# Causal Toeplitz filters: one quarter by three block products, both lags in one matmul, with the second layer's work in other steps

## The chip, the cores and the metric

The kernel runs on one core of a Trainium2 chip. The metric is the device time of one execution in microseconds (us), median of repeated runs. The core's engines each have an instruction queue of their own, taken in order: TensorE (PE, matmuls; PEld is its load of weights), VectorE (DVE), ScalarE (ACT), GpSimd (POOL) and SyncE (SP, which only issues DMAs here). They wait for each other by semaphores. Everything is float32.

## The reference

Two "metaformer" layers on x of shape (8, 128, 32, 32), so 8 images of 1024 tokens with 128 channels. What matters here is the token mixer of layer 0 and what comes after it:

```python
x = x + attention(ln_c(x))                    # layer 0, first half
t = to_tokens(x)
t = t + stu(ln_t(t))                          # layer 0, second half: the filters
x = from_tokens(t)
x = x + deformable_conv(ln_c(x))              # layer 1, first half: gathers
t = t + experts(ln_t(t))                      # layer 1, second half: top 2 of 8 experts

def stu(u):                                   # for 4 resolutions, mixed by weights
    U_plus  = causal_convolution(phi_k, u)            # 16 filters k, each over all tokens
    U_minus = sgn * causal_convolution(phi_k, sgn * u)  # sgn = +1, -1, +1, ...
    out = sum_k s_k * (U_plus_k @ Mpp_k + U_minus_k @ Mpm_k)
    return out + sum_{i<3} shift(u, i) @ Mu_i
```

With the signs, the sum and the difference of U_plus and U_minus need only tokens of equal or of unequal parity. So tokens are split into even and odd ones, 512 of each, and a filter into its even and its odd lags. One filter then is, for each image, four causal convolutions of length 512: from each source parity to each result parity. Each is a product with a lower triangular Toeplitz matrix of 512 x 512.

## The kernel before

The kernel has three stages: attention (to about 911 us), the filters with the second layer of earlier images beside them (to about 2743 us), and the second layer of the last two images alone.

**Filter stage** (`spectral_and_second_layer`). Images go in four groups of two. The loop runs over 64 items of work, (group, filter k) with 16 filters to a group. One iteration does the convolutions of its own item and the mix of the item before. For each of the 4 pairs (result parity, term) and each of 2 images, `filter_image` (L1366 to L1378) computes a convolution by four matmuls into one PSUM bank `pu`: the weights are a tile of 128 source tokens (`ur`, of which `xc` and `ht` are other names in the even groups), the moving operand is a piece of the filter's Toeplitz rows (`teto`, or `hk` for the first filter), of 512, 384, 256 and 128 columns. That is the lower triangle in 10 blocks of 128 x 128. ACT copies the bank to `us` (L1378). Two banks take turns as `pu`.

`mix` multiplies the `us` of the item before by its matrices `mf` and accumulates in four banks `po` (L1362), for 512 columns after each image's convolution. The mix is cut in SPANS, since the four resolutions reach over different numbers of tokens. At a group's first filter `start_sums` begins `po` with the residual and the three lags `mu`. At its last, `finish` copies `po` to `x2`.

In the first group, `load_matrices` makes `mf` from M_plus and M_minus: a sum and a difference on POOL (L1274, L1275), four weightings on DVE (L1279, L1281), and a write to HBM, from where later groups load it. `lags` makes `mu` in the same way (L1248, L1250).

**Work beside it.** The second layer of the previous group's two images, and the preparation of the next group, are generators in a list `behind`. After each image's convolution and piece of mix, `advance(2.6)` takes steps from the list until they add up to that many units (a step that yields no number counts 1). So what order the engines' queues have is written out by hand. A step's instructions stand in the queue of each engine behind all that came ahead in the program. An image's steps are: transposes back to tokens, norm (`norm_steps`: statistics on DVE, an inverse root by Newton steps on POOL, scaling on DVE, L793), a matmul with the convolution's matrices (L1015), its result written to a table in HBM (24 DMAs from SP), `corners` (indices and weights of the bilinear samples), 24 points, each an indirect DMA on POOL (L1065) and four multiply-adds on DVE (L1078), a norm, `gates` (the top two experts), and 16 expert steps of one matmul (L1096) and four multiply-adds on DVE (L1102). Next comes the preparation of the next group: load, norm, and `channels` (p_ut, L1318). What is left of it at the group's end is done at once.

In the last stage, the two images of the last group run the same steps, interleaved with each other (`alone`).

**What sets buffers free.** The filter tile `teto` has three buffers, `mf` three, the gathered rows `g` nine.

Of the kernel before, what the change touches and what calls it, by code (L numbers as in the profile page):

```python
# [34 lines left out]
GROUPS = ((0, 1), (2, 3), (4, 5), (6, 7))  # L35
RATE = (2.6, 3.5)
STAGGER = 16
# [363 lines left out]
class BoundedAttention:  # L401
# [6 lines left out]
    def __init__(self, nc, cp):  # L408
        self.nc = nc
        HG, NH = self.HG, self.NH  # L410
        self.xc = cp.tile([P, T], F32, name="xc")
        self.ht = cp.tile([P, NT, C], F32, name="ht")
        self.hk = cp.tile([P, 2 * HT + 2], F32, name="hk")
        self.wq = cp.tile([C, HG, NH, 32], F32, name="wq")
        self.wk = cp.tile([C, HG, NH, 32], F32, name="wk")
        self.wv = cp.tile([C, C], F32, name="wv")
        self.group = cp.tile([P, NG], F32, name="group")
        self.spread = cp.tile([P, 2, P], F32, name="spread")
        self.pick = cp.tile([P, HG, NH, HD], F32, name="pick")
# [381 lines left out]
class DeformAndExperts:  # L801
# [182 lines left out]
    def image(self, b, x2, alone):  # L984
# [8 lines left out]
        hc = sb.tile([C, T], F32, tag="hc", name="hc")  # L993
        yield from self.turn_steps(ht, hc)
        yield

# [48 lines left out]
        idx, w = got  # L1045
        nc.gpsimd.tensor_tensor(tok, tok, self.cb.unsqueeze(1).to_broadcast([P, NT, C]), ALU.add)
        x3 = sb.tile([P, NT, C], F32, tag="x3", name="x3")
# [6 lines left out]
        def fetch():  # L1054
            if len(fetched) < len(points):
                i, tap = points[len(fetched)]
                if alone:
                    at = idx[:, i, tap : tap + 1]
                else:
                    if tap == 0:  # L1060
                        here.append(sb.tile([P, TAPS], I32, tag="here", name="here", bufs=3))
                        nc.scalar.copy(here[-1], idx[:, i, :])  # L1062
                    at = here[-1][:, tap : tap + 1]
                g = sb.tile([P, 4 * C], F32, tag="g", name="g", bufs=9)
                nc.gpsimd.indirect_dma_start(  # L1065
                    out=g, out_offset=None, in_=rows,
                    in_offset=bass.IndirectOffsetOnAxis(ap=at, axis=0),
                )
                fetched.append(g)

        for _ in range(3):
            fetch()
        yield
        yield
# [60 lines left out]
    def gates(self, tt, got):  # L1135
# [23 lines left out]
        yield  # L1159
        oh2 = self.first_max(e2, "b")  # L1160
        nc.vector.tensor_add(oh1, oh1, oh2)
        gates = sb.tile([P, P // NE, NE], F32, tag="gates", name="gates")
# [14 lines left out]


def read_filter(nc, t, phi_e, phi_o, k):
    nc.sync.dma_start(t[:, 0:HT], bass.AP(phi_e.tensor, k * PHI_ROW, [[1, P], [1, HT]]))  # L1180
    nc.sync.dma_start(
        t[:, HT : 2 * HT + 1], bass.AP(phi_o.tensor, k * PHI_ROW, [[1, P], [1, HT + 1]])
    )
    return t[:, 0:HT], t[:, HT : 2 * HT + 1]

# [32 lines left out]
class Spectral:  # L1218
# [4 lines left out]
    def __init__(self, ctx, tc, dram, phi_e, phi_o, M_u, M_plus, M_minus, coef, x1d, back, given):  # L1223
        nc = self.nc = tc.nc
        cp = ctx.enter_context(tc.tile_pool(name="s_const", bufs=1))
        self.sb = ctx.enter_context(tc.tile_pool(name="s_sb", bufs=1))
        self.up = ctx.enter_context(tc.tile_pool(name="s_u", bufs=2, space=PSUM))
        self.op = ctx.enter_context(tc.tile_pool(name="s_o", bufs=1, space=PSUM))
# [12 lines left out]

    def lags(self, w):
        nc = self.nc
        for f in range(NFR):
            m = self.sb.tile([C, TAPS, C], F32, tag="m_u", name="m_u")
            nc.sync.dma_start(m, self.M_u[f].rearrange("i d e -> d i e"))
            if f == 0:
                nc.vector.tensor_scalar(self.mu[:, f], m, w[:, f : f + 1], None, ALU.mult)  # L1248
            else:
                nc.vector.scalar_tensor_tensor(  # L1250
                    self.mu[:, f], m, w[:, f : f + 1], self.mu[:, f - 1], ALU.mult, ALU.add
                )

    def load_filter(self, k):


        t = self.sb.tile([P, 2 * HT + 1], F32, tag="teto", name="teto", bufs=3)
        return read_filter(self.nc, t, self.phi_e, self.phi_o, k)

    def load_matrices(self, k, first):  # L1260

        nc, sb = self.nc, self.sb
        mf = sb.tile([C, NFR, 2, C], F32, tag="mf", name="mf", bufs=3)
        if not first:
            nc.sync.dma_start(mf, self.mfd[k])
            return mf
        mp = sb.tile([C, NFR, C], F32, tag="mp", name="mp")
        mm = sb.tile([C, NFR, C], F32, tag="mm", name="mm")  # L1270
        nc.sync.dma_start(mp, self.M_plus[:, k].rearrange("f d e -> d f e"))
        nc.sync.dma_start(mm, self.M_minus[:, k].rearrange("f d e -> d f e"))
        both = sb.tile([C, NFR, 2, C], F32, tag="both", name="both")
        nc.gpsimd.tensor_add(both[:, :, 0, :], mp, mm)  # L1274
        nc.gpsimd.tensor_sub(both[:, :, 1, :], mp, mm)  # L1275
        for f in range(NFR):
            by = self.coef[:, f, k : k + 1]
            if f == 0:
                nc.vector.tensor_scalar(mf[:, f], both[:, f], by, None, ALU.mult)  # L1279
            else:  # L1280
                nc.vector.scalar_tensor_tensor(  # L1281
                    mf[:, f], both[:, f], by, mf[:, f - 1], ALU.mult, ALU.add
                )
        nc.sync.dma_start(self.mfd[k], mf)
        return mf

    def prepare(self, group):

        nc, sb = self.nc, self.sb
        group["x1"], group["ur"] = [], []  # L1290
        for n, b in enumerate(group["images"]):
# [7 lines left out]
            if group["number"] % 2:  # L1299
                group["ur"].append(sb.tile([P, NT, C], F32, tag="ur", name="ur", bufs=2))  # L1300
            else:
                group["ur"].append(self.given.ur[n])
        group["ut"] = sb.tile([C, 2, 2, HT + 1], F32, tag="ut", name="ut")

    def normal(self, group, newton):

        for x1, ur in zip(group["x1"], group["ur"]):
            yield from norm_steps(self.nc, self.sb, x1, ur, 1e-5, newton)

    def channels(self, group, bank):  # L1310
# [55 lines left out]

    def filter_image(self, group, n, par, term, teto, us):

        nc = self.nc
        src = par if term == 0 else 1 - par  # L1370
        flt = teto[0] if term == 0 else teto[1][:, par : par + HT]
        pu = self.up.tile([P, HT], F32, tag="u", name="pu")
        for i in range(4):
            nc.tensor.matmul(  # L1374
                pu[:, i * P : HT], group["ur"][n][:, src * 4 + i, :], flt[:, 0 : HT - i * P],
                start=(i == 0), stop=(i == 3),
            )
        nc.scalar.copy(us[:, n, :], pu)  # L1378

    def mix(self, group, par, term, spans, mf, us, last):  # L1380
        for lo, hi, k in spans:
            self.add(
                group, (par, lo // 256), self.span(group, par, lo, hi), mf[:, k - 1, term, :],
                us[:, 0 : len(group["images"]), lo:hi], last and term == 1,
            )
# [11 lines left out]
def spectral_and_second_layer(tc, spec, layer, weights):  # L1397
    groups = [{"images": im, "number": g} for g, im in enumerate(GROUPS)]
    work = [(g, k) for g in range(len(groups)) for k in range(NF)]
    spec.prepare(groups[0])  # L1400
    filters = {0: spec.given.filter, 1: spec.load_filter(1)}
    matrices = {0: spec.load_matrices(0, True)}
    spec.lags(weights)
    matrices[1] = spec.load_matrices(1, True)

# [16 lines left out]
    for n in range(len(work) + 1):  # L1422
# [9 lines left out]
        if now is not None and now[1] == 0 and now[0]:  # L1432
            for _ in starts[now[0]]:
                pass
        if n + 2 < len(work):
            filters[n + 2] = spec.load_filter(work[n + 2][1])
        sums = {}
        for i in range(4 if now or before else 0):
            par, term = divmod(i, 2)
            if now is not None:  # L1440
                group = groups[now[0]]
                us = spec.sb.tile([C, 2, HT], F32, tag="us", name="us", bufs=6)
                sums[i] = us
            for m in range(2):
                unit = now is not None and m < len(group["images"])
                if unit:
                    spec.filter_image(group, m, par, term, filters[n], us)
                if before is not None:
                    if before[1] == 0 and i + m == 0:
                        spec.start_sums(groups[before[0]])  # L1450
                    spec.mix(
                        groups[before[0]], par, term, SPANS[0:3] if m == 0 else SPANS[3:4],
                        matrices[n - 1], kept[i], before[1] == NF - 1,
                    )
                if unit:
                    advance(RATE[2 - len(group["images"])])
        if before is not None and before[1] == NF - 1:
            spec.finish(groups[before[0]])
        if n + 2 < len(work):
            matrices[n + 2] = spec.load_matrices(work[n + 2][1], work[n + 2][0] == 0)  # L1460
        kept, before = sums, now
    while behind:
# [106 lines left out]
```

## Time and profile before

| what | value |
|---|---|
| time, median of 3 runs | 2969.61 us (2966.56 to 2971.4) |
| span of the profiled run | 2966.7 us, 45298 instructions |
| PE busy | 2759.9 us, 93% |
| DVE, ACT, POOL busy | 1405.6, 982.0, 976.3 us |
| filter matmuls (L1374), share of the chain | 35% |
| mix and start of the sums (L1362), share of the chain | 16% |
| DMA | 199.80 MB, mean 67 GB/s |

The chain is the chain of work that ended last, followed back from the last instruction to whatever released each step. Busy time of PE overstates: its matmuls are pipelined and their ends are modelled, so the busy times of neighbours overlap. A matmul in float32 shows as two instructions.

The costliest rows that the change touches (line, engine, operation, tiles, count, busy us, mean ns of one, idle time of the engine before them and what ended it):

```profile
L1378 ACT COPY us<-pu 128x512 f32<-128x512 f32 x512 | 299.4, 585 | 1301.1 <-PE pu L1374 1266.9
...
L1374 PE MATMUL pu<-teto,ur 128*128 128x512 f32 (+3 forms) x2048 | 594.4, 433 | 0.0
...
L1078 DVE SCALAR_TENSOR_TENSOR x<-g,w,x 128x128 f32<-128x128 f32 x704 | 250.0, 356 | 43.0 <-DMA g<-tab,here 11.5
L1102 DVE SCALAR_TENSOR_TENSOR x<-p_e,gates,x 128x128 f32<-128x128 f32 x512 | 177.7, 350 | 188.7 <-PE p_e L1096 172.4
```

ACT sat idle ahead of the copies of `pu` until PE had written them: it waited for PE, not the other way round.

### The profile page before, as it was taken

What the parts mean: (1) busy time and instruction counts of PE and PEld (TensorE: products, weight loads), DVE (VectorE), ACT (ScalarE), POOL (GpSimd) and SP (SyncE); (2) the same over time, 40 slices, a digit from 0 to 9 for tenths busy, and PEclk for the clock granted to TensorE, in tenths of its full rate; (3) what the DMA queues carried; (4) which work ended last, traced back from release to release, by engine and by line L of the source; (5) the groups of instructions that cost most, each with busy time, mean ns of one, the idle gap of its engine ahead of it and who ended that gap; (6) DMA issues with size and microseconds to landing.
All of it is one profiled execution on the core that took longest, in us unless ns stands there. A gap on an engine that the chain in (4) does not pass through costs nothing.

```text
span 2966.7 us, 45298 instructions
## 1 busy us (share of the span) xinstructions
PE 2759.9 (93%) x18896; PEld 1693.4 (57%) x18896; DVE 1405.6 (47%) x2882; ACT 982.0 (33%) x1246; POOL 976.3 (33%) x977
## 2 busy tenths in 40 slices
PE   7999999999998999999999999999999999999316
PEld 3555555555555666666666666666666666666103
DVE  4888888888882200000432532333333153333586
ACT  4666667676661111112212111221211221221100
POOL 4777777777881211100200301210210030220230
PEclk9999999999998999999999999999999999999658
DMA  1000000000002322221614411521621441530730
GB/s 27 2 16 16 2 16 16 2 16 9 16 16 83 101 64 64 64 61 51 184 39 128 143 35 36 170 82 41 191 64 36 116 135 34 157 99 8 229 112 15
DMA packets 177012, 199.80 MB, mean 67 GB/s; under 512 B 17237, under 2 KB 135189, under 8 KB 176801
## 3 DMA queue, kind: packets, MB, share of 16 engines
q1 hardware_dynamic: 147328, 134.97, 15.3%
q0 software_dynamic: 16800, 55.59, 6.1%
q10 hardware_dynamic: 12672, 6.29, 0.7%
q8 instruction: 150, 2.46, 0.3%
q14 instruction: 62, 0.50, 0.1%
HBM read 128.88 MB, written 67.92 MB: 66 GB/s over the span
## 4 chain that ended last, share of the span: by engine, by line
PE 58%; DVE 6%; DMA 1%; issue 1%; POOL 0%; ACT 0%; SPq 0%; DVEq 0%; POOLq 0%; ACTq 0%
PE pu L1374 35%; PE po L1362 16%; PE p_e L1096 3%; DVE x L1078 2%; PE p_g L1015 1%; DVE x L1102 1%; DMA tab<-gs 1%; PE p_out L1113 0%; PE p_turn L918 0%; PE p_out L1116 0%; PE p_l L1140 0%; DVE st L785 0%; DVE mv L786 0%; PE p_ut L1318 0%; DMA g<-tab,cn_idx 0%
## 5 line engine op out<-in xcount | busy, mean ns | idle before, releaser
L1378 ACT COPY us<-pu 128x512 f32<-128x512 f32 x512 | 299.4, 585 | 1301.1 <-PE pu L1374 1266.9
L620 POOL TENSOR_TENSOR t<-e 128x1024 f32<-128x1024 f32 x256 | 607.9, 2375 | 199.4 <-ACT e L611 199.2
L648 DVE TENSOR_TENSOR e<-e,rb 128x2048 f32<-128x2048 f32 x256 | 570.8, 2279 | 83.6 <-PE rb L641 83.6
L1374 PE MATMUL pu<-teto,ur 128*128 128x512 f32 (+3 forms) x2048 | 594.4, 433 | 0.0
L611 ACT ACTIVATE e<-s 128x2048 f32<-128x2048 f32 x256 | 480.9, 1879 | 253.2 <-PE s L606 251.3
L1374 PEld LDWEIGHTS pu<-teto,ur 128*128 128x128 f32 x2048 | 386.5, 190 | 273.0 <-issue 185.1
L1362 PE MATMUL po<-us,mf 128*128 128x128 f32 (+2 forms) x2048 | 528.1, 381 | 0.0
L606 PE MATMUL s<-q,k 32*128 32x256 f32 x4096 | 296.1, 403 | 14.0 <-ACT e L611 13.2
L658 PE MATMUL av<-e,vt 128*32 128x256 f32 x4096 | 290.0, 391 | 2.9 <-DVE e L648 1.6
L1374 PE MATMUL pu<-teto,xc 128*128 128x512 f32 x992 | 290.5, 436 | 0.0
L1374 PE MATMUL pu<-teto,ht 128*128 128x512 f32 x992 | 287.7, 433 | 0.0
L1065 POOL DMA_INDIRECT g<-tab,here x144 | 137.6, 956 | 447.0 <-ACT here L1062 252.8
L1374 PEld LDWEIGHTS pu<-teto,xc 128*128 128x128 f32 x992 | 189.0, 191 | 153.9 <-issue 114.2
L1362 PEld LDWEIGHTS po<-us,mf 128*128 128x128 f32 x2048 | 270.9, 192 | 4.1 <-issue 3.9
L1078 DVE SCALAR_TENSOR_TENSOR x<-g,w,x 128x128 f32<-128x128 f32 x704 | 250.0, 356 | 43.0 <-DMA g<-tab,here 11.5
L1102 DVE SCALAR_TENSOR_TENSOR x<-p_e,gates,x 128x128 f32<-128x128 f32 x512 | 177.7, 350 | 188.7 <-PE p_e L1096 172.4
L606 PEld LDWEIGHTS s<-q,k 32*128 32x128 f32 x4096 | 186.4, 185 | 136.9 <-ACT e L611 115.7
L1374 PEld LDWEIGHTS pu<-teto,ht 128*128 128x128 f32 x992 | 187.7, 190 | 110.0 <-issue 64.7
L770 POOL TENSOR_SCALAR rs_v<-rs_v 128x8 f32<-128x8 f32 x18 | 4.4, 245 | 711.3 <-DVE rs_b L768 711.3
L658 PEld LDWEIGHTS av<-e,vt 128*32 128x32 f32 x4096 | 101.7, 109 | 141.4 <-issue 85.2
L1096 PE MATMUL p_e<-ew,tc 128*128 128x512 f32 x256 | 133.1, 626 | 15.4 <-DVE x L1102 10.3
L634 DVE RECIPROCAL r<-z 128x256 f32<-128x256 f32 x64 | 112.5, 1757 | 69.0 <-PE z L627 68.8
(237 smaller groups left out, 1829.0 us busy)
## 6 DMA issues: line engine op xcount, KB each, us to landing
tab<-gs SPq DMA_DIRECT2D x168, 256.0 KB
mf<-mfd SPq DMA_DIRECT2D x48, 512.0 KB
teto<-in_phi_o SPq DMA_DIRECT2D x63, 256.5 KB
teto<-in_phi_e SPq DMA_DIRECT2D x63, 256.0 KB
mfd<-mf SPq DMA_DIRECT2D x16, 512.0 KB
tab<-gs ACTq DMA_DIRECT2D x24, 256.0 KB
xc<-in_x SPq DMA_DIRECT2D x8, 512.0 KB
x1d<-xt SPq DMA_DIRECT2D x8, 512.0 KB
```

The source lines that it names most:

```text
L606: nc.tensor.matmul(s[:, j, c, :], img["k"][rows, hg, 2 * r + c, :], q[rows, qc * QU : (qc + 1) * QU], start=True, stop=True,)
L611: nc.scalar.activation(e.rearrange("p j c q -> p (j c q)"), s.rearrange("p j c q -> p (j c q)"), AF.Exp, scale=float(HD) ** -0.5,)
L620: nc.gpsimd.tensor_add(t, e[:, :, 0, :], e[:, :, 1, :])
L648: nc.vector.tensor_tensor(e, e, un["rb"].unsqueeze(2).to_broadcast([P, NH, 2, QU]), ALU.mult)
L658: nc.tensor.matmul(qrt["av"][32 * j : 32 * j + 32, 0:QU], img["v"][:, 2 * r + c, P * hg + 32 * j : P * hg + 32 * j + 32], un["e", r][:, j, ...
L1065: nc.gpsimd.indirect_dma_start(out=g, out_offset=None, in_=rows, in_offset=bass.IndirectOffsetOnAxis(ap=at, axis=0),)
L1078: nc.vector.scalar_tensor_tensor(x3[:, i, :], fetched[n][:, k * C : (k + 1) * C], w[:, i, tap, k : k + 1], (tok if tap + k == 0 else x3)[: ...
L1096: nc.tensor.matmul(pe, tc[:, i * P : (i + 1) * P], self.ew[:, grp * 4 : grp * 4 + 4, :].rearrange("d e c -> d (e c)"), start=True, stop=True,)
L1102: nc.vector.scalar_tensor_tensor(x3[:, i, :], pe[:, k * C : (k + 1) * C], gate[:, i, grp * 4 + k : grp * 4 + k + 1], x3[:, i, :], ALU.mult ...
L1362: self.nc.tensor.matmul(out, lhsT, rhs, start=bank not in group["opened"], stop=last, skip_group_check=True)
L1374: nc.tensor.matmul(pu[:, i * P : HT], group["ur"][n][:, src * 4 + i, :], flt[:, 0 : HT - i * P], start=(i == 0), stop=(i == 3),)
L1378: nc.scalar.copy(us[:, n, :], pu)
```

## The change

**Fewer block products.** The Toeplitz matrix of a causal convolution of length 512 in blocks of 128 has T0 on the diagonal, then T1, T2, T3 below it. Its lower left quarter is T2 x0 + T1 x1 (third result tile) and T3 x0 + T2 x1 (fourth). It is now computed as T2 (x0 + x1), shared by both, plus (T1 - T2) x1 and (T3 - T2) x0: three products for four. The sums of source tiles (`sum`, `add_tiles`, DVE) are made once per group, the differences of filter blocks (`diff`, `differences`, POOL) once per item, in the iteration before it. A convolution now has 9 blocks for 10.

**Both lags in one matmul.** The even and the odd lags meet the same source tile, so their columns lie side by side: a matmul's moving operand is two strips of 128 (or of 256) columns out of the filter tile, its result two strips of a bank. A unit is now (source parity, image), four in an iteration instead of eight. The bank `high` takes result tiles 2 and 3 of both lags, the bank `low` first the shared product and then result tiles 0 and 1; each has one buffer. ACT copies the shared product to `us_w`, DVE adds it to `high` on its way to `us`, ACT copies `low`.

**Pieces and steps.** The first group's matrices and `mu` are made in pieces, spread over the iteration's units, within the item's own iteration and not two ahead. `teto` and `mf` have two buffers, loaded at the end of an iteration; the loads of M_u have no tile of their own. The mix is as before, in two parts after each unit, each followed by `advance(2.85)`. The first four gathers of an image stand in steps of 1.3 with pauses, one more ahead than before; `g` has seven buffers; `gates` has one more step; the bias of the convolution is added earlier.

```diff
-RATE = (2.6, 3.5)
+RATE = 2.85
...
+        nc.gpsimd.tensor_tensor(tok, tok, self.cb.unsqueeze(1).to_broadcast([P, NT, C]), ALU.add)
         yield
...
-        nc.gpsimd.tensor_tensor(tok, tok, self.cb.unsqueeze(1).to_broadcast([P, NT, C]), ALU.add)
...
-                g = sb.tile([P, 4 * C], F32, tag="g", name="g", bufs=9)
+                g = sb.tile([P, 4 * C], F32, tag="g", name="g", bufs=7)
...
-        for _ in range(3):
+        for n in range(3 if alone else 4):
             fetch()
+            if not alone:
+                yield 1.3
...
         oh2 = self.first_max(e2, "b")
+        yield
...
-        self.up = ctx.enter_context(tc.tile_pool(name="s_u", bufs=2, space=PSUM))
+        self.up = ctx.enter_context(tc.tile_pool(name="s_u", bufs=1, space=PSUM))
...
-        t = self.sb.tile([P, 2 * HT + 1], F32, tag="teto", name="teto", bufs=3)
-        return read_filter(self.nc, t, self.phi_e, self.phi_o, k)
+        return read_filter(
+            self.nc, self.sb.tile([P, FILTER], F32, tag="teto", name="teto", bufs=2),
+            self.phi_e, self.phi_o, k,
+        )
+
+    def differences(self, t):
...
+        d = self.sb.tile([P, 5 * DIFF], F32, tag="diff", name="diff", bufs=2)
+        for lags, width in enumerate((P, P + 1)):
+            at = HT * lags
+            nc.gpsimd.tensor_sub(
...
-        mf = sb.tile([C, NFR, 2, C], F32, tag="mf", name="mf", bufs=3)
+        mf = sb.tile([C, NFR, 2, C], F32, tag="mf", name="mf", bufs=2)
...
+        return mf, [terms, partial(weigh, (0, 1)), partial(weigh, (2, 3))]
...
+    def add_tiles(self, group):
+
+        for ur, both in zip(group["ur"], group["sum"]):
+            halves = ur.rearrange("p (par i) c -> p par i c", par=2)
+            self.nc.vector.tensor_add(both, halves[:, :, 0, :], halves[:, :, 1, :])
...
-        src = par if term == 0 else 1 - par
-        flt = teto[0] if term == 0 else teto[1][:, par : par + HT]
-        pu = self.up.tile([P, HT], F32, tag="u", name="pu")
-        for i in range(4):
-            nc.tensor.matmul(
-                pu[:, i * P : HT], group["ur"][n][:, src * 4 + i, :], flt[:, 0 : HT - i * P],
-                start=(i == 0), stop=(i == 3),
-            )
-        nc.scalar.copy(us[:, n, :], pu)
...
+        pw = bank("low")[:, :, 0:P]
+        product(pw, group["sum"][n][:, src, :], blocks(2 * P, 3 * P), True, True)
+        w = self.sb.tile([C, 2, P], F32, tag="us_w", name="us_w", bufs=2)
+        nc.scalar.copy(w, pw)
+        tile = [ur[:, src * 4 + i, :] for i in range(4)]
+        high = bank("high")
+        product(high, tile[2], blocks(0, 2 * P), True)
+        product(high[:, :, 0:P], tile[1], less(0))
+        product(high[:, :, P:], tile[0], less(1))
+        product(high[:, :, P:], tile[3], blocks(0, P), False, True)
+        nc.vector.tensor_tensor(
+            us[:, :, n, 2 * P :].rearrange("c two (b t) -> c two b t", b=2),
+            high.rearrange("c two (b t) -> c two b t", b=2),
+            w.unsqueeze(2).to_broadcast([C, 2, 2, P]), ALU.add,
+        )
+        low = bank("low")
+        product(low, tile[0], blocks(0, 2 * P), True)
+        product(low[:, :, P:], tile[1], blocks(0, P), False, True)
+        nc.scalar.copy(us[:, :, n, 0 : 2 * P], low)
...
+                if now is not None:
+                    spec.filter_image(group, m, src, filters[n], less[n], us)
+                    if src + m == 0 and n + 1 < len(work):
+                        less[n + 1] = spec.differences(filters[n + 1])
+                    for make in (pieces, matrices[n][1]):
+                        if 2 * src + m < len(make) and make[2 * src + m]:
+                            make[2 * src + m]()
...
+                    if now is not None:
+                        advance(RATE)
...
         if n + 2 < len(work):
-            matrices[n + 2] = spec.load_matrices(work[n + 2][1], work[n + 2][0] == 0)
-        kept, before = sums, now
+            filters[n + 2] = spec.load_filter(work[n + 2][1])
+        if n + 1 < len(work):
+            matrices[n + 1] = spec.load_matrices(work[n + 1][1], work[n + 1][0] == 0)
+        kept, before, pieces = sums, now, []
```

## The prediction, made before the changed kernel ran

> **What bounds the kernel now.** I read the slices of the span first, to find stages. TensorE (PE) is at 9 tenths from the attention to slice 37 at a granted clock of 9 tenths; the end is VectorE's (DVE).
>
> ```profile
> PE   7999999999998999999999999999999999999316
> DVE  4888888888882200000432532333333153333586
> ...
> PEclk9999999999998999999999999999999999999658
> ```
>
> The table of windows says how full PE is in the four groups of the filter stage (columns: length, then busy us of PE, PE's weight loads, DVE, ScalarE (ACT), GpSimd (POOL), clock, DMA share, GB/s).
>
> ```profile
> 1000.00:1430.00 430.00, 425.71 (x1718) 278.84 (x1717) 36.98 (x109) 86.16 (x152) 40.00 (x52) 0.99 0.25 71
> 1430.00:1880.00 450.00, 441.88 (x1809) 288.14 (x1808) 159.56 (x546) 92.48 (x176) 66.35 (x131) 0.99 0.28 85
> 1880.00:2320.00 440.00, 431.88 (x1779) 282.44 (x1778) 158.85 (x547) 88.53 (x171) 64.05 (x119) 0.99 0.32 97
> 2320.00:2745.00 425.00, 422.35 (x1704) 272.39 (x1703) 151.09 (x512) 88.94 (x173) 61.53 (x104) 1.00 0.31 93
> ```
>
> The idle rests of PE are 4.3, 8.1, 8.1 and 2.7 us: 23 us of 1745. DVE is busy 29% of the stage, ACT and POOL less. Then the chain of waits in a quiet stretch of the first group, for what one unit costs; busy sums of matmuls overlap, this chain doesn't.
>
> ```profile
> 1086.00 2.16 PE pu L1374 x8
> 1088.16 0.86 PE po L1362 x2
> 1089.02 2.16 PE pu L1374 x8
> 1091.18 0.88 PE po L1362 x6
> ```
>
> One filter unit (four matmuls, each shown as two instructions, of 512+384+256+128 = 1280 columns) takes 2.16 us, so 1.69 ns a column, and the mix of 512 columns after it 0.87 us. Nothing stands between. An iteration is eight such pairs, 24.2 us; 64 iterations are 1550 us, over half of the span. **In this stage only PE's columns count.**
>
> **What the skill says.** (1) The Trainium skill, "TensorE: Matmul & The Clock Gate", section Back-to-back issue gap: the gap between matmuls grows with the columns N and little else (262 cycles for 256, 518 for 512). The trace agrees: 0.88 us for a mix cut into matmuls of 128, 128 and 256 columns, 0.86 us for one of 512. (2) "Perfetto Trace Analysis", section Matmuls: independent matmul groups should rotate through PSUM banks, so that one is evacuated while the next is computed. The trace shows this working: no wait of PE on a copy of ACT after L1374. The change alters the rotation. (3) "SBUF — State Buffer", section Who interferes with whom: a DVE operation with at most one SBUF input, outside the two-port modes, doesn't contend with GpSimd. The new addition reads one operand in PSUM; no run shows it yet.
>
> **The change, part by part.**
>
> *Products (filter_image).* Before, one iteration has 2 parities x 2 terms x 2 images x 1280 = 10240 columns. After, a unit is a source parity of an image with both lags side by side: 256 (sum of two tiles) + 512 + 3 x 256 into bank "high", then 512 + 256 into bank "low": 2304. Four units make 9216. Saved: 1024 columns x 1.69 ns = 1.73 us per iteration, x 64 = **110.6 us**. The moving operands become two strips of 128. The mix already reads and writes strips of two images at 1.70 ns a column, so I price the strides at nothing. Small tiles are no longer used: no matmul is under 256 columns. The mix keeps its 16 x 256 columns.
>
> *Evictions.* Before, eight ACT copies of 512 (585 ns) per iteration. After, per unit: an ACT copy of 256 (0.37 us, as the copy of the same shape at L668), a DVE addition of 512 out of PSUM, and an ACT copy of 512. ACT falls from 4.7 to 3.8 us per iteration. The DVE addition is not in the trace of before: the nearest row, the PSUM copy of 512 at L1394, is 0.69 us; the price in "VectorE: DVE Perf Modes", section on the TRN2 errata, is (120 + 512) cycles at 0.96 GHz, an estimate of 0.66 us. I take 0.69; 4 x 64 of them are 177 us, in a stage where DVE idles over 1200 us. Hidden in amount. In order of time: a unit is PE 0.43 (sum), 2.16 (high), 1.30 (low), then 0.87 + 0.87 of mix.
> The high bank is free for 1.30 + 1.74 + 0.43 = 3.47 us from its last matmul to its next use; the addition needs 0.69. The low bank has 2.16 us for the 0.37 us copy and 1.74 us for the 0.59 us copy. So all fit with over a microsecond of reserve, if the engine is at hand.
>
> *The new wait.* Bank "high" now waits for DVE, whose queue is in order and holds the second layer's work. Ahead of an addition stand at worst: four multiply-adds of a gather point (4 x 353 ns = 1.41 us), up to two expert steps (2.8 us, whose PE part ran before the unit), or a normalisation that waits 3.5 us for POOL. The first is inside 3.47 - 0.69 = 2.78 us of slack. Expert steps are the same length as the slack, but begin before the unit's 2.59 us up to the end of "high". The POOL wait begins three steps ahead, over half a unit. I book 5 us for those that miss.
> Gathers: L1078 waits for its data mostly in steps of three, and the data land 3.5 to 6 us after the issue (issues at 1454.21, use at 1457.69; 1473.68 and 1474.92, use from 1480.74). After the change a gather is asked for four points ahead, 10.4 of the scheduler's units, or 10 us at 2.82 us per step of 2.85: landed in time. The first gather of an image waited for the table's writes until 1426.53 and its use began at 1431.64; the new pauses between fetches give it 5.2 units more. Hidden.
>
> *Expert matmuls.* Two steps can now be emitted, then 0.87 us of mix, then two more, over two banks that DVE frees in 1.41 us each: the fourth waits some 0.3 us. 96 steps in 6 images, 3.35 to a unit, 29 units: up to 9 us; I take 5.
>
> *Rates.* Counting yields, an image costs 152.8 units before and 159.0 after; an iteration spends 8 x 2.6 = 20.8 before and 8 x 2.85 = 22.8 after. Before, 23 of 31 steps of the next group's preparation are left at the boundary and forced at once: PE's waits of 6.2 us for DVE before p_ut, at two boundaries. After, 7 are left, with the normalisation emitted. Saved: 10 us of 12.4.
>
> *Start of the stage.* Before, start_sums waited 3.6 us for mu and 2.1 us for POOL; both go (-5.7). New: the first "high" needs the differences, behind two indirect loads on POOL that ended at 916; 2 x 0.73 us more (as L683, 256 elements) is 917.5, where PE arrives at 912.5: +5. Iteration 0 has no mix to hide the low copy: +2. DVE's base (L856), which sat 16 us for a small DMA, now stands ahead of an addition; its DMA is also asked for earlier: +5 (0 to 10). Together +6.
>
> *Hidden.* POOL's differences in the other iterations (1.5 us, an iteration ahead; POOL is 15% busy), matrices in three pieces (same operations), filters in two buffers (loaded at an iteration's end, used an iteration later: 22 us for 0.5 MB), the earlier addition of the bias on POOL, seven gather buffers in place of nine.
>
> *Sum:* 2969.6 - 110.6 - 10 + 6 + 5 + 5 = **2865 us**.
>
> **The rivals.**
> *DVE's queue on PE's path.* For: every unit now waits for an engine that waits for DMA, ACT, POOL and PE. Against: the slack above. If half of the 192 units of the last three groups lose 0.4 us, that is +38: 2903; with the same on all, up to 2945. 17%.
> *Evictions exposed (slower).* One buffer each for high and low instead of two for one tag. Break-even is 110.6 / 256 = 0.43 us per unit. If each unit bares one addition of 0.69 us, 256 x 0.69 = 177, so 2969.6 - 110.6 + 177 = 3036. Against: over a microsecond of independent mix stands in between. 9%.
> *No gain:* strips cost PE as much as the columns save: about 2967. 3%.
>
> **How the numbers follow.** The forecast has 71%. Its low end is all waits gone and no new one: 2969.6 - 110.6 - 12.4 - 5.7 = 2841, so 2843; its high end, with base at 10, experts at 9 and 15 of misses, is near 2884. To leave out no more than 2 in 10 the range takes in the DVE case to 2910. Faster 0.88, same 0.03, slower 0.09.
>
> **What would show it.** Right: the chain shows units near 3.89 us of pu and 0.87 us of mix, PE's stage from 911 (first unit) to 2743 (end of the last mix) shortened by some 100 us, PE idle still under 30 us in it, the DVE addition near 0.7 us, and p_ut waits of 6.2 us gone. Wrong: a line of PE waiting for the addition or for ACT's copy of w in most units, a unit clearly over 3.89 us without waits (strips), or p_e waiting for DVE by tens of us. The tail from the end of the last group should stay at some 223 us.

## The result and the profile after

The changed kernel takes 2894.28 us (median of 4 runs, 2889.07 to 2896.89), the kernel before 2968.49 us beside it: a ratio of 0.9747, 95% interval 0.973 to 0.9764. That is 74 us less. It lies inside the stated range and 29 us above the forecast time. It also lies above 2884 us, the high end that the forecast's own terms gave; the range reached further only because it took in the rival of DVE's queue.

The slices of the span have the same shape as before: PE full, then a short end.

```profile
PE   7999999999997999999999999999999999999316
```

The chain of waits in a quiet stretch of the first group (start, us, what) shows the new unit.

```profile
1063.86 0.43 PE pu_low L1435 x2
1064.29 2.15 PE pu_high L1435 x8
1066.44 1.29 PE pu_low L1435 x4
1067.73 1.74 PE po L1406 x8
```

The products of a unit take 3.87 us and its two parts of mix 1.74: 5.61 us. Two of the old pairs took 6.06 us (1086.00 to 1091.18 + 0.88). So the products cost what their columns say, strips and all.

The groups of the page (line, engine, tiles, count, busy us, mean ns, idle before and what ended it) show the evictions.

```profile
L1447 DVE TENSOR_TENSOR us<-pu_high,us_w 128x512 f32<-128x512 f32 x256 | 176.9, 691 | 680.4 <-PE pu_high L1435 680.4
...
L1455 ACT COPY us<-pu_low 128x512 f32<-128x512 f32 x256 | 149.8, 585 | 834.6 <-PE pu_low L1435 834.6
...
L1435 PE MATMUL pu_high<-teto,ur 128*128 128x512 f32 (+1 forms) x512 | 212.6, 497 | 19.7 <-DVE us L1447 19.7
...
L1440 ACT COPY us_w<-pu_low 128x256 f32<-128x256 f32 x256 | 95.4, 373 | 419.2 <-PE pu_low L1435 333.4
```

The addition takes 691 ns, the copy 373, as forecast. The third row is new: PE sat idle before `pu_high` for DVE. The windows of the four groups (length, busy of PE, PEld, DVE, ACT and POOL, clock, DMA share, GB/s) show how much in all.

```profile
1000.00:1330.00 330.00, 330.00 (x1312) 227.79 (x1311) 62.61 (x112) 57.82 (x120) 54.22 (x56) 1.00 0.25 70
1330.00:1790.00 460.00, 446.75 (x1786) 301.52 (x1785) 212.13 (x636) 83.98 (x188) 93.41 (x165) 0.98 0.34 96
1790.00:2230.00 440.00, 425.22 (x1695) 286.22 (x1694) 209.29 (x632) 80.54 (x182) 91.92 (x163) 0.98 0.34 98
2230.00:2670.00 440.00, 428.90 (x1713) 288.10 (x1712) 197.48 (x577) 79.16 (x179) 82.71 (x132) 0.98 0.34 95
```

In the first group, which has no second layer beside it, PE doesn't idle at all after 1000 us. In each of the others it idles 11 to 15 us, more than the 3 to 8 us of before. Together that is 39 us, where the prediction's sign of being right was under 30. From its first unit to the end of the last mix the stage took 1757 us in place of 1832: 75 us less, not some 100. PE's waits from 1000 to 2670 us (what it waited for: us in total, times, longest) name it.

```profile
PE pu_high L1435 <- DVE us L1447: 31.2, 6, 6.4
PE p_ut L1362 <- DVE ht L793: 2.3, 1, 2.3
PE p_ut L1362 <- DVE ur L793: 2.3, 1, 2.3
PE p_gt L1175 <- DVE gates L1171: 1.0, 3, 0.3
...
PE p_e L1098 <- DVE x L1104: 1.0, 3, 0.3
```

Six waits, and six images have their second layer in this stretch: one wait to an image. The timelines around the first of them (start, us, engine, line, operation, tiles; idle before it and its releaser) are, of ACT, POOL, SP, DVE and PE:

```profile
1383.07 0.19 ACT L1062 COPY here<-cn_idx 128x3 int32<-128x3 int32 x1 [0.46 <-DVE cn_idx L967]
```

```profile
1391.77 1.07 POOL L1065 DMA_INDIRECT g<-tab,here  x1 [15.53 <-DMA teto<-in_phi_e]
```

```profile
1363.74 4.15 SPq L1009 DMA_DIRECT2D tab<-gs  x6
1370.14 17.92 SPq L1009 DMA_DIRECT2D tab<-gs  x18
```

```profile
1386.30 0.69 DVE L1447 TENSOR_TENSOR us<-pu_high,us_w 128x512 f32<-128x512 f32 x1 [1.88 <-PE pu_high L1435]
1397.43 0.71 DVE L1080 SCALAR_TENSOR_TENSOR x<-g,w,tok 128x128 f32<-128x128 f32 x1 [10.44 <-DMA g<-tab,here]
1398.18 1.82 DVE L1080 SCALAR_TENSOR_TENSOR x<-g,w,x 128x128 f32<-128x128 f32 x3
1399.91 0.68 DVE L1447 TENSOR_TENSOR us<-pu_high,us_w 128x512 f32<-128x512 f32 x1
```

```profile
1394.67 0.59 PE L1435 MATMUL pu_low<-teto,sum 128*128 128x256 f32 x2
1400.65 2.07 PE L1435 MATMUL pu_high<-teto,ur 128*128 128x512 f32 x2 [5.39 <-DVE us L1447]
```

The indices were there at 1383.07, but POOL issued the first gather at 1391.77. The releaser printed there is the DMA that came last by the profile; what the gather needs of a DMA is the table, whose 24 writes SP issued from 1363.74 to 1388.06; experiment 7 shows that this is the wait. DVE stood at the first point from 1386.99 to 1397.43. Behind that point in its queue was the addition that frees bank `high`, and behind that bank stood PE.

### The profile page after: what moved, and what is told of

The parts are those of the page before. It is cut to its first block, busy times and chain, and to the rows that moved or that the text cites. A ratio compares the mean times of both kernels' runs of the same rounds, so it can differ in the third digit from the quotient of the medians.

```text
span 2891.4 us, 44980 instructions
## 1 busy us (share of the span) xinstructions
PE 2666.7 (92%) x18384; PEld 1674.4 (58%) x18384; DVE 1588.8 (55%) x3146; ACT 926.5 (32%) x1246; POOL 1072.5 (37%) x1105
## 4 chain that ended last, share of the span: by engine, by line
PE 80%; DVE 7%; issue 3%; DMA 3%; SPq 2%; POOL 2%; ACT 2%; DVEq 0%; POOLq 0%; ACTq 0%
PE pu_high L1435 18%; PE po L1406 15%; PE pu_low L1435 13%; PE s L606 9%; PE av L658 8%; PE z L627 4%; PE p_e L1098 3%; DVE x L1080 2%; PE rb L641 2%; SPq L1009 2%; DVE x L1104 1%; ACT e L611 1%; PE p_g L1016 1%; PE pq L561 1%; PE pk L575 1%
## 5 line engine op out<-in xcount | busy, mean ns | idle before, releaser
L1447 DVE TENSOR_TENSOR us<-pu_high,us_w 128x512 f32<-128x512 f32 x256 | 176.9, 691 | 680.4 <-PE pu_high L1435 680.4
L1406 PE MATMUL po<-us,mf 128*128 128x128 f32 (+2 forms) x2048 | 496.1, 381 | 0.0
L1455 ACT COPY us<-pu_low 128x512 f32<-128x512 f32 x256 | 149.8, 585 | 834.6 <-PE pu_low L1435 834.6
L1279 POOL TENSOR_TENSOR diff<-teto 128x256 f32<-128x256 f32 x126 | 92.4, 739 | 854.9 <-DMA teto<-in_phi_e 758.0
L1406 PEld LDWEIGHTS po<-us,mf 128*128 128x128 f32 x2048 | 307.6, 191 | 44.8 <-issue 21.9
L1435 PE MATMUL pu_high<-teto,ur 128*128 128x512 f32 (+1 forms) x512 | 212.6, 497 | 19.7 <-DVE us L1447 19.7
L1440 ACT COPY us_w<-pu_low 128x256 f32<-128x256 f32 x256 | 95.4, 373 | 419.2 <-PE pu_low L1435 333.4
L1435 PE MATMUL pu_low<-teto,ur 128*128 128x512 f32 (+1 forms) x512 | 186.5, 487 | 0.0
L1435 PEld LDWEIGHTS pu_low<-teto,sum 128*128 128x128 f32 x504 | 94.2, 191 | 108.1 <-issue 105.6
L1435 PE MATMUL pu_low<-teto,sum 128*128 128x256 f32 x504 | 150.5, 380 | 0.7 <-ACT us L1455 0.7
```

The lines of the kernel that those rows point to most:

```text
L1406: self.nc.tensor.matmul(out, lhsT, rhs, start=bank not in group["opened"], stop=last, skip_group_check=True)
L1435: nc.tensor.matmul(out, weights, moving, start=start, stop=stop, skip_group_check=True)
L1447: nc.vector.tensor_tensor(us[:, :, n, 2 * P :].rearrange("c two (b t) -> c two b t", b=2), high.rearrange("c two (b t) -> c two b t", b=2) ...
L1455: nc.scalar.copy(us[:, :, n, 0 : 2 * P], low)
```

## The experiments

Beside the experiments the kernel before took 2965.8 to 2966.1 us, beside the changed kernel 2968.5. So a difference of an experiment from the changed kernel is good to some 3 us.

**1. The columns alone.** To the kernel before:

```diff
-        for i in range(4):
+        for i in range(3):
```

with the group's end moved to the third matmul (`stop=(i == 2)`). The last block of each triangle is left out.

> The kernel before, with the fourth matmul of each convolution (128 columns) left out, so the last block of each Toeplitz product is missing: 8 x 128 = 1024 columns fewer per iteration, as many as the change saves, and no new wait on DVE. Theory (only PE's columns count, 1.69 ns each, 64 iterations): 110 to 113 us less than before, 2857 us. Rival (a part of PE's time hangs on something other than columns, so the missing 30 us were never there to win): 2875 us or more.

Measured: 2856.74 us against 2966.05, a ratio of 0.9634 (0.9618 to 0.965): 109.3 us less. The first term of the sum, 110.6 us, is right to 1%. The rival falls: all of it was there to win.

**2. The other steps alone.** To the kernel before, the new rate, pauses, longer gates, earlier bias and seven gather buffers:

```diff
-RATE = (2.6, 3.5)
+RATE = (2.85, 3.5)
...
-        for _ in range(3):
+        for n in range(3 if alone else 4):
             fetch()
+            if not alone:
+                yield 1.3
...
-                g = sb.tile([P, 4 * C], F32, tag="g", name="g", bufs=9)
+                g = sb.tile([P, 4 * C], F32, tag="g", name="g", bufs=7)
```

> The kernel before with the other steps alone: 2.85, pauses between four first gathers, the longer gates, the earlier bias, seven gather buffers; the products as they were. Theory (the steps matter only at the two group boundaries, where PE waited 6.2 us each for normalisation): 8 to 12 us less than before, 2955 to 2959 us. Rival (the steps in themselves bring a good part of the gain): 2945 us or less.

Measured: 2950.86 us against 2965.96, a ratio of 0.9943 (0.9928 to 0.9958): 15 us less, between the two. From one start of sums to the next it takes 464.0 us (1359.81 to 1823.77) where the kernel before takes 472.8 (1358.22 to 1830.99). From there to the third start it takes 463.97 us for 471.92. So the two waits of 6.2 us, which are gone, cost 8.8 and 8.0 us: in the kernel before, PE's clock was 0.56 and 0.59 in the windows from 1797 to 1801 and from 1801 to 1805 us, at the end of the first of them and after it. Some 1.6 us were lost ahead of the first start, where PE now waited 8.1 us for `ur` at one place.

With experiment 1 this makes 124 us: 2844 us (2968.5 - 124.4) is what the two gains would give if nothing were lost. The changed kernel is 50 us above that.

**3. DVE off PE's path.** To the changed kernel:

```diff
-        nc.vector.tensor_tensor(
-            us[:, :, n, 2 * P :].rearrange("c two (b t) -> c two b t", b=2),
-            high.rearrange("c two (b t) -> c two b t", b=2),
-            w.unsqueeze(2).to_broadcast([C, 2, 2, P]), ALU.add,
-        )
+        nc.scalar.copy(us[:, :, n, 2 * P :], high)
```

> The changed kernel, with the bank high copied by ACT and the addition of the shared product left out, so the results of tiles 2 and 3 lack one term; PE's work is the same, DVE is off PE's path. Theory (six waits of PE for the addition, 4.3 to 6.4 us each, which stands behind the first gather of each image in DVE's queue, and the low clock after each, some 2.6 us): 45 us less than the changed kernel, 2849 us, and no wait of pu_high over 1 us from 1000 us on. Rival (the missing 30 us are spread over strips, expert steps and the start of the stage): 2885 us or more.

Measured: 2830.64 us against 2966.05, a ratio of 0.954 (0.9525 to 0.9556), so 64 us less than the changed kernel, more than I expected. PE's waits from 1000 to 2596 us are down to one line, and its window to one microsecond of idle time (length, busy of PE, clock, DMA share, GB/s).

```profile
PE p_e L1098 <- DVE x L1104: 1.0, 3, 0.3
```

```profile
1300.00:2596.00 1296.00, 1295.04 (x5256) 1.00 0.36 101
```

The rival falls. Expert steps, strips and evictions on ACT cost PE next to nothing here. Between the profiled executions, 59 us of the gain lie in the three groups, where the six waits account for 44 (below); over half of the rest are the two waits for `ht` and `ur`, gone here, with the slow stretches after them. Another 5.5 us lie ahead of the first start of sums (1320.37 us for 1325.90), where PE had waited 4.6 us for additions, mostly for one behind `base`. The end, after the last mix, was 3.5 us longer.

**4 and 5. Longer pauses, and their control.** To the changed kernel, both with `RATE = 2.95`, and one of them with

```diff
-        yield
-        yield
+        for _ in range(2 if alone else 6):
+            yield
```

> The changed kernel with six empty steps in place of two between an image's first gathers and its first point, and 2.95 in place of 2.85 so that the group's work still fits. Theory (DVE comes to the first point too early, and the addition of the next unit stands behind it): the addition passes first, the six waits shrink to under 1 us, 2850 to 2858 us. Rival (the additions are held up wherever the gather stands, since the gather comes later too): no gain, 2890 to 2900 us.

> The changed kernel with 2.95 in place of 2.85 alone, the control for the run with longer pauses. Theory (the table's writes take their 22 us however fast the steps are emitted, so a faster rate brings DVE to the first point 3.5% earlier): each of the six waits 0.5 to 1 us longer, 2896 to 2902 us. Rival (the rate itself is what helps in the run with pauses): 2880 us or less.

Measured: 2864.78 us with pauses (0.9663, 0.9647 to 0.9679) and 2906.56 us with the rate alone (0.9805, 0.9788 to 0.9821). The pauses gain 30 us on the changed kernel, 42 on their control. PE's waits of the control, then of the run with pauses:

```profile
PE pu_high L1435 <- DVE us L1447: 43.2, 6, 9.6
PE p_gt L1175 <- DVE gates L1171: 11.3, 6, 1.9
```

```profile
PE pu_high L1435 <- DVE us L1447: 11.9, 5, 3.7
PE pu_low L1435 <- ACT us_w L1440: 4.3, 3, 1.6
```

The pauses help as the theory has it, though the time is 7 us above the expected range; the control is 5 us above its own. With pauses, the first image of each group is free of the wait (at most 1.3 us), but the second, which now begins at another point of the iteration, still waits 2.9 to 3.7 us. In the control the waits grew by 2 us on average, not 1, and not evenly: those of the first images stayed as they were (4.8, 5.8 and 5.4 us for 5.4, 6.4 and 5.1), those of the second images grew to 8.2 to 9.6 us from 4.3 to 5.0. So the theory of a rate 3.5% faster doesn't explain the control. Where in the iteration an image begins seems to matter more; no run isolates it.

**6. The pauses taken away,** and with them the fourth of the first gathers. To the changed kernel:

```diff
-        for n in range(3 if alone else 4):
+        for _ in range(3):
             fetch()
-            if not alone:
-                yield 1.3
```

> The changed kernel with three first gathers and no pauses between them, as before. Theory (the pauses hide 5.2 of the steps' units, near 5 us, of each image's first gather): each of the six waits about 5 us longer, 2920 to 2935 us. Rival (the pauses only shift the wait): 2885 to 2900 us.

Measured: 2916.68 us (0.9836, 0.9821 to 0.9851), 22 us more than the changed kernel and a little less than expected. The wait doubles, by 5.0 us for each image on average (4.2 to 5.9), as the theory has it:

```profile
PE pu_high L1433 <- DVE us L1445: 61.1, 6, 11.6
```

So the pauses of the change already hide half of the wait that the change opens. The six waits grew by 30 us, the time by 22: the two waits of 2.3 us at the group boundaries are not in this run's list, nor the slow stretches after them.

**7. A table for each tap.** The gather of a point waits for all that was written to its table. To the changed kernel:

```diff
-            tab = dram.tile([TAPS, self.ROWS, 4, C], F32, name=f"tab{n}")
+            tab = [dram.tile([self.ROWS, 4, C], F32, name=f"tab{n}_{i}") for i in range(TAPS)]
...
-        rows = tab.rearrange("t r s c -> (t r) (s c)")
+        rows = [part.rearrange("r s c -> r (s c)") for part in tab]
...
-                    out=g, out_offset=None, in_=rows,
+                    out=g, out_offset=None, in_=rows[tap],
```

with the index's offset by tap and the writes' targets to match.

> The changed kernel with a table of its own for each tap, so that the first gather waits for 16 of the 24 writes. Theory (the wait is for the table's writes): first gather issued 6 to 8 us earlier, the six waits of pu_high under 1 us, 2848 to 2860 us. Rival (the gather is late since its own 256 KB stand among the writes in busy DMA engines, at 250 to 310 GB/s in this stretch): it lands where it did, 2885 us or more.

Measured: 2839.78 us against 2965.96, a ratio of 0.9575 (0.956 to 0.959): 54.5 us less than the changed kernel, and 8 us under the expected range. The timelines of POOL and DVE at the same image:

```profile
1382.86 1.07 POOL L1065 DMA_INDIRECT g<-tab,here  x1 [9.66 <-DMA tab<-gs]
1385.86 0.96 POOL L1065 DMA_INDIRECT g<-tab,here  x1 [1.92 <-DMA tab<-gs]
1389.99 0.95 POOL L1065 DMA_INDIRECT g<-tab,here  x1 [3.18 <-DMA tab<-gs]
```

```profile
1387.79 0.35 DVE L1080 SCALAR_TENSOR_TENSOR x<-g,w,tok 128x128 f32<-128x128 f32 x1 [2.91 <-DMA g<-tab,here]
1388.17 1.13 DVE L1080 SCALAR_TENSOR_TENSOR x<-g,w,x 128x128 f32<-128x128 f32 x3
1389.80 0.69 DVE L1447 TENSOR_TENSOR us<-pu_high,us_w 128x512 f32<-128x512 f32 x1 [0.50 <-PE pu_high L1435]
```

The gather goes 9 us earlier (7 us, counted from the group's start of sums, which itself came 2.1 us earlier), each tap as its own writes land; the addition waits for PE again, and no wait of `pu_high` is left from 1000 to 2600 us. This is the cause, taken away by itself. The rival falls: among busy DMA engines the gather still landed some 5 us after its issue.

**8. The same mend before the change.** Experiment 7's edit in the kernel before:

> The kernel before with a table for each tap and nothing else. Its DVE also sat 9 us for the first gather, but nothing of PE stood behind it. Theory (the wait costs only since the addition put DVE's queue on PE's path): the same time as before, 2963 to 2969 us. Rival (the earlier gathers are a gain in themselves): 2940 us or less.

Measured: 2963.3 us against 2965.76, a ratio of 0.999 (0.9982 to 0.9998): 2.5 us. The same wait for the same writes was there and cost nothing to speak of; only the addition's place made it dear.

**9 and 10. The addition after the bank is free.** To the changed kernel, on DVE and on POOL (whose edit is shown); in both, `us_w` has four buffers in place of two:

```diff
-        nc.vector.tensor_tensor(
-            us[:, :, n, 2 * P :].rearrange("c two (b t) -> c two b t", b=2),
-            high.rearrange("c two (b t) -> c two b t", b=2),
-            w.unsqueeze(2).to_broadcast([C, 2, 2, P]), ALU.add,
-        )
+        nc.scalar.copy(us[:, :, n, 2 * P :], high)
+        part = us[:, :, n, 2 * P :].rearrange("c two (b t) -> c two b t", b=2)
+        nc.gpsimd.tensor_tensor(
+            part, part, w.unsqueeze(2).to_broadcast([C, 2, 2, P]), ALU.add
+        )
```

> The changed kernel with ACT copying the bank high to us, and DVE adding the shared product afterwards in SBUF (us_w with four buffers). All products and sums are done; DVE has as much to do as in the changed kernel and stands as long behind the first gathers, but PE's bank no longer waits for it, only the mix half an iteration later (11 us or more). Theory (the bank held through DVE's queue is the whole cost): as without the addition, 2828 to 2838 us. Rival (DVE's lateness reaches PE through us and the mix as well): 2870 us or more.

> The same with the addition on POOL, which stands some 8 us behind the table's writes at each image's first gather. Theory (any engine that frees the bank late costs, any engine after the bank is free doesn't): 2830 to 2842 us, a little of it from POOL and DVE reading SBUF at once. Rival (POOL's wait for the writes, longer than DVE's, reaches the mix): 2860 us or more.

Measured: 2852.42 us on DVE (0.9614, 0.9601 to 0.9627), 2835.41 us on POOL (0.9562, 0.9549 to 0.9575). POOL is as expected, though its addition takes 1271 ns where DVE's takes 691. DVE is 14 us above the range. The six waits are gone there too, but smaller ones remain (from 1000 to 2620 us):

```profile
PE p_gt L1175 <- DVE gates L1171: 4.1, 6, 0.9
PE p_ut L1362 <- DVE ht L793: 3.2, 1, 3.2
PE p_ut L1362 <- DVE ur L793: 3.2, 1, 3.2
PE p_turn L918 <- DVE tt L793: 2.9, 6, 0.5
```

So the bank is most of the cost, not the whole: additions also push the second layer's own steps back on DVE, and PE has matmuls of those in its queue. The four lines make 13.4 us of the 22 us between this run and experiment 3, and 3.7 us lie ahead of the first start of sums (1324.08 us for 1320.37). The rest I haven't traced.

**11. Both mends.** Experiments 7 and 10 together:

> The changed kernel with both mends: a table for each tap, and the addition on POOL after ACT has freed the bank. Theory (the two take away the same cost, so they don't add up): 2828 to 2835 us, at most 8 us better than the addition on POOL alone (2835). Rival (they act on different waits): 2820 us or less.

Measured: 2829.78 us against 2965.76, a ratio of 0.9541 (0.9528 to 0.9554). This beats both kernels, by 64.5 us the changed one. The two mends alone gave 54.5 and 59 us; together they don't add up, so it is one cost that both take away.

## Why the prediction was right, and where it was off

**Products** (-110.6 us): right, 109.3 measured alone. What the term rests on is the trace's 1.69 ns a column; the cycles that the prediction quotes from the Trainium skill are, in that section, those of an isolated matmul, and the section gives others for a stream.

**Evictions** (hidden): right in size, 691 and 373 ns against 0.69 and 0.37 us, and right in the first group after 1000 us, where DVE had little else. Whether POOL holds up an addition with one operand in PSUM, which no run had shown, can be read now: between 1330 and 2600 us the additions took 670 to 694 ns, also those that ran beside POOL's differences.

**Gathers** (hidden, 0 us): this step failed, and it is more than the whole gap. The prediction saw that the first gather of an image waits for the table's writes, set against it that the pauses "give it 5.2 units more", and booked nothing. Measured: six waits of 4.3 to 6.4 us, 31.2 us in all, and after each a slow stretch of PE. Three things were wrong with that. First, the size of the wait was never reckoned. In the kernel before, DVE stood 9.09 us at the first image's first point, and 5.2 units are some 5 us. What is left is above the 2.78 us of slack that the prediction had worked out, and so it is for the first image of each group (8.6 to 10.8 us). For the second images (5.8 to 6.0 us) it would have been below.

```profile
1399.78 0.93 SPq L1008 DMA_DIRECT2D tab<-gs  x2
```

```profile
1431.64 0.35 DVE L1078 SCALAR_TENSOR_TENSOR x<-g,w,tok 128x128 f32<-128x128 f32 x1 [9.09 <-DMA g<-tab,here]
```

Second, the steps go faster than before: 24.2 us for 20.8 units was 1.16 us a unit, 22.4 us for 22.8 units is 0.98. From SP's first write to the moment when DVE stood ready at the first point it took 22.8 us before (1399.78 to 1422.55) and takes 23.3 now (1363.74 to 1386.99), with the pauses in it. So the pauses only made up for the pace. Third, the writes don't get faster with the steps: from the first write to the first gather's issue it took 26.75 us before (to 1426.53) and takes 28.0 now (to 1391.77), with the DMA engines busy at a share of 0.85 to 1.07 and 250 to 313 GB/s in the windows from 1364 to 1388 us. The time from issue to landing was right (3.5 to 6 us; here 5.7). So DVE's wait didn't shrink, it was 10.44 us, and PE's bank now stands behind it. Before, the same wait was harmless (experiment 8).

**The clock after a wait** was in no term. After each of the six waits the rest of the products took 5.24 to 5.92 us instead of 3.44: 1.8 to 2.5 us, 13.2 in all. The windows around the first show why (length, busy of PE, clock, DMA share, GB/s).

```profile
1385.00:1395.00 10.00, 10.00 (x42) 1.00 0.90 252
1395.00:1400.50 5.50, 0.26 (x2) 0.82 0.74 258
1400.50:1403.00 2.50, 2.35 (x4) 0.50 0.48 128
1403.00:1406.00 3.00, 3.00 (x8) 0.60 0.70 201
```

The Trainium skill, "TensorE: Matmul & The Clock Gate", section What's actually happening, says that an idle window of about 3.4 us takes the array back to half its clock until it has been busy for as long. The trace agrees for these waits: the clock is 0.50 after 5.4 us of idling. But here a shorter wait could do it too. The wait of 2.30 us for `ht` in the changed kernel, which ended at 1752.92 us, was followed by 0.50; the same wait of 2.30 us in experiment 7, ended at 1735.82 us, by 1.00 (changed kernel, then experiment 7).

```profile
1752.00:1754.00 2.00, 0.94 (x4) 0.88 0.35 141
1754.00:1756.00 2.00, 2.00 (x11) 0.50 0.00 0
```

```profile
1736.00:1738.00 2.00, 1.87 (x14) 1.00 0.00 0
```

So the six waits cost 31.2 + 13.2 = 44.4 us, and experiment 7, which takes them away, shortens the three groups by 46.4 us (457.4, 457.7 and 421.2 us before it, from sums to sums or to the last mix, 441.1, 442.5 and 406.2 after). That is more than the gap of 29 us. Other terms came out better than booked, as the next ones show; that the time stayed this near to the forecast is in part luck.

**Rates** (-10): the forced waits of 6.2 us fell to 2.3 each. Alone the steps gave 15 us, since the term left out the low clock after the waits; in the changed kernel two waits of 2.3 us were left, with slow stretches after them. **Expert matmuls** (+5): 1.0 us measured; two banks suffice. **Missed additions** (+5): none but those at first gathers. **Start of the stage** (+6): some 3 us. PE had five units, the sums and 1024 columns of mix done at 963.65 us, the kernel before as much at 962.90, and the 2.3 us of columns saved by then belong to the first term. The wait for the differences was 1.0 us, not 5, since PE had first waited 5.3 us for `sum`, which the prediction didn't list; the low copies made 2.0 us, as booked, and the wait behind `base` 3.8 of the 5. **The tail**: 220.6 us against 223.4; over all runs it lies between 215.8 and 224.1, so these 3 us can't be put down to the change.

The rival of DVE's queue on PE's path is what happened. It had the right mechanism with 17% and 2903 us, yet put it evenly on half of the units at 0.4 us (on all of them that makes 2942 us, not 2945). It was six events of 7.4 us. The rival of bared evictions and that of dear strips fell with experiments 3 and 1.

## What to carry to other kernels

When an eviction moves to an engine with other work in its queue, its duration and the engine's load say little: look up the longest wait that stands in that queue, even one that cost nothing so far, and ask whether the bank's reserve covers it. If it doesn't, let an engine with a quiet queue free the bank and do the arithmetic afterwards, or shorten the wait (here a table cut in three, so that a reader waits only for its own part). Where a faster stage runs beside transfers that don't get faster with it, pauses reckoned at the slower stage's pace no longer cover them.

## What the hardware showed that I had not expected

- A wait of PE of 4.3 to 6.4 us costs 1.8 to 2.5 us more through the clock; in experiment 2, taking away two waits of 6.2 us gained 8.8 and 8.0 us. A wait of 2.30 us lowered the clock in one run and not in another.
- POOL's addition of 512 elements out of SBUF took 1271 ns, 1.8 times DVE's (692), and cost the kernel less, since PE shows no wait for it.
- It wasn't free for DVE. Its multiply-adds on gathered rows, with two operands in SBUF, took 375 ns on average in the changed kernel and 546 with the addition on POOL (experiment 10); those of the expert steps, with one operand in PSUM, took 350 in both (from 1330 to 2560 us; the lines are the changed kernel's, then experiment 10's).

```profile
L1080 DVE SCALAR_TENSOR_TENSOR x<-g,w,x 128x128 f32<-128x128 f32 x517 | 193.9, 375 | 16.8
```

```profile
L1080 DVE SCALAR_TENSOR_TENSOR x<-g,w,x 128x128 f32<-128x128 f32 x528 | 288.2, 546 | 18.7
```
